# A graph network layer: eight buffers of gathered rows in place of six, and half the descriptor ring

## The chip, the cores and the metric

The kernel runs on one core of one Trainium2 chip. The metric is the device time of one execution in microseconds (us); a comparison rests on the median of several runs.

## The reference

One layer of message passing over 12500 nodes of 64 features and 412500 edges of 32 features, sorted by receiver. Cut to what is computed (`act` is `x * sigmoid(x)`):

```
h = maximum(layernorm(x), 0)
msg_in = concat(h[src], h[dst], edge)                  # 64 + 64 + 32 per edge
messages = act(msg_in @ W1 + b1) @ W2 + b2
logits = act(msg_in @ Wa1 + ba1) @ Wa2 + ba2
messages = messages * softmax(logits, axis=0)          # over all edges
aggregated = segment_sum(messages, dst)
out = x + act(concat(h, aggregated) @ Wu1 + bu1) @ Wu2 + bu2
```

## The kernel before

**Prologue.** The nodes are normalised in chunks, and two tables are written to memory: `ts_d`, each node's share of both first layers as a sender (128 numbers, 512 bytes a row), and `tr_d`, the same as a receiver. The stores of `tr_d` are L415; the sums ahead of them are the lines L412 on VectorE, from two tiles `tr` that take turns.

**Main loop (`one_pass`).** The edges, in order of their receivers, are cut into 403 groups of 1024 (eight columns of 128). `load(g)` runs two groups ahead of the group that is worked on. It fetches, on SyncE, a window of `tr_d` (tile `wins`, three buffers), and every fourth group edge features and receivers (`eo`, `dbs`), and computes with TensorE (L659) into PSUM `pe` what edge and receiver give. The senders' rows come by indirect DMAs of GpSimd, one for each column of 128 edges (L630), into a buffer `gs` of the pool `gather`. `begin(g)` adds `gs` to `pe` on VectorE (L678, and L680 or L682 for the last column) and applies tanh on ScalarE (L683); this reading is what frees the buffer. `end(g)` makes messages and logits, and `sum_up` adds up a group some iterations back (L764 copies its result out of PSUM).

Not every column is gathered by GpSimd. In the groups `chosen` (every even one from 10 to 390) ScalarE copies the senders' 128 columns one by one out of `hT` in SBUF (L570), in four parts of 32 over the two iterations that begin four before the group; the copies take their addresses from registers that are loaded from a list of byte addresses (L562). In the groups `rowed` (g mod 8 = 1, from 17 to 377) SyncE fetches the 128 rows one by one, 16 in each iteration (L600). Those groups have seven gathers, the others eight.

**What sets the order.** Nearly all instructions of the engines are pinned in the order in which the program writes them. The gathers are in the program's order on GpSimd's queue, and each waits for its buffer. As GpSimd has no other work, it runs ahead of the loop as far as buffers allow. The pool `gather` has six buffers of 4 KB per partition. The first two are taken before the loop by `raws`, the nodes' rows of groups 0 to 3, so groups 4 to 7 get the next four, groups 8 and 9 wait until `raws` is used up, and from group 10 on the gathers of group g wait for `begin(g - 6)`.

At the start of each SBUF partition lies the ring in which GpSimd writes the descriptors of its DMAs, 16 KB by default, and 128 bytes of constants; then comes `hT`, the first tile. `HOME = 16512` is therefore the byte address of `hT`, and the lists of addresses hold `4 * column + HOME`:

```
pin(nc.vector.tensor_scalar(to, to, 4.0, float(HOME), op0=ALU.mult, op1=ALU.add))
...
pin(nc.scalar.copy(to[:, at:at + 4], hb[:, bass.ds(regs[i] - HOME, 4)]))
```

**End.** The last groups have no columns by ScalarE and no single rows. Then the sums are turned into the update, whose inputs (`bs`, `xs`, L811 and L812) for the last five of 13 parts lie in buffers of the pool `gather` too.

Of the kernel before, what the change touches and what calls it, by code (L numbers as in the profile page):

```python
# [76 lines left out]
EVERY = 4  # L77
LEADS = {0: 8, 2: 8}
SLOTS = ((0, 32), (32, 32), (64, 32), (96, 32))
HOME = 16512  # L80
FIRST = 10
ROWS = 16
SPAN = -(-EP // ROWS)
# [16 lines left out]
def gnn_kernel(ctx: ExitStack, tc: tile.TileContext, n_edges, x, src, src_row, dst, dst_row, first, edge,  # L100
               weights, out):
    nc = tc.nc
# [90 lines left out]
    wrong = const.tile([EP, 1], I32, name="wrong")  # L193


    gather = ctx.enter_context(tc.tile_pool(name="gather", bufs=6))


    with tc.tile_pool(name="node1", bufs=1) as node1, \
# [281 lines left out]
def one_pass(tc, n_edges, v):  # L481
# [18 lines left out]
    with ExitStack() as ctx:  # L500
# [13 lines left out]
        with tc.tile_pool(name="work2", bufs=2) as work2, \  # L514
# [9 lines left out]
            def column_lists():  # L524

                m = NB // 2
                for i, (r, gs) in enumerate(of_phase.items()):
# [12 lines left out]
                    pin(nc.vector.scalar_tensor_tensor(to, to, float(P), near, op0=ALU.mult, op1=ALU.add))  # L540
                    pin(nc.vector.tensor_scalar(to, to, 4.0, float(HOME), op0=ALU.mult, op1=ALU.add))
                    pin(nc.vector.tensor_scalar(num, num, 1, None, op0=ALU.bitwise_and))
# [15 lines left out]
            def columns(g, first, n):  # L558
                if first == 0:
                    cols[g] = small.tile([P, EP], F32, name="cols", bufs=2)  # L560
                to = cols[g].bitcast(U8)
                loads, regs = nc.values_load_multi_w_load_instructions(  # L562
                    lists[g][0:1, first:first + n], engines=[ENG.Activation], min_val=HOME,
                    max_val=HOME + 4 * (NP // 2 - 1),
                    skip_runtime_bounds_check_because=WHY)
                for one in loads:
                    pin(one)
                for i in range(n):
                    at = 4 * (first + i)
                    pin(nc.scalar.copy(to[:, at:at + 4], hb[:, bass.ds(regs[i] - HOME, 4)]))  # L570

# [674 lines left out]
```

## Time and profile before

| | |
|---|---|
| median of 3 runs (lowest, highest) | 6093.8 us (6085.5, 6116.05) |
| profiled execution, as a whole | 6095.58 us |
| its span, first to last instruction | 6093.9 us |
| mean granted TensorE clock | 0.593 |
| busy: TensorE, VectorE, ScalarE, GpSimd | 38%, 47%, 52%, 47% |
| moved by DMA | 387.82 MB, 64 GB/s on average |

In the profile PE is TensorE's matmuls, PEld its weight loads, DVE VectorE, ACT ScalarE, POOL GpSimd, SP SyncE (SPq its queue). L630 is line 630 of the kernel. A group of instructions is told by its line, engine and operation, then "written tile <- tiles read". What stands behind "<-" in a wait is what the engine waited for last; "issue" is idle time in which it waited for nothing that the profile shows, and "remote" a release that the profile can't name.

### The profile page before, as it was taken

How to read it: one execution, taken by the hardware profiler on the slowest of the kernel's cores; microseconds unless marked ns; L12 is line 12 of the kernel's file. 1: busy time of each engine (PE TensorE's matmuls, PEld its weight loads, DVE VectorE, ACT ScalarE, POOL GpSimd, SP SyncE). 2: the span in 40 equal slices, each digit the busy share in tenths (PEclk: the TensorE clock that was granted, in tenths of full speed). 3: DMA queues.
4: the chain of work that ended last, by engine and by line, in shares of the span. 5: the costliest groups of instructions: out<-in, count | busy, mean ns of one | idle time of the engine just before them, and what ended most of it. 6: DMA issues, size and time to landing. Idle time of an engine off the chain costs nothing. (4 is left out here: it accounts for less than half of the span.)

```text
span 6093.9 us, 81385 instructions
## 1 busy us (share of the span) xinstructions
PE 2340.9 (38%) x11616; PEld 1926.1 (32%) x11616; DVE 2856.1 (47%) x6971; ACT 3176.7 (52%) x25258; POOL 2843.3 (47%) x3012
## 2 busy tenths in 40 slices
PE   4333334434333343344434433333333333333345
PEld 3333233323333232233323333332323322322334
DVE  4444444445444444445444444444444444444446
ACT  2455555555555555555555555555555555555531
POOL 4544444444444444445445444444444544444443
PEclk6666555555555555655556665566556666555656
DMA  4222222222222221222222222222222212122222
GB/s 172 66 68 53 61 59 62 68 56 66 62 59 63 53 67 52 66 56 67 62 53 70 56 68 55 62 63 53 66 56 62 65 52 57 53 53 60 61 72 67
DMA packets 238362, 387.82 MB, mean 64 GB/s; under 512 B 77789, under 2 KB 167368, under 8 KB 224760
## 3 DMA queue, kind: packets, MB, share of 16 engines
q1 hardware_dynamic: 142232, 187.67, 12.0%
q0 software_dynamic: 95584, 194.90, 11.8%
q14 instruction: 451, 3.69, 0.2%
q8 instruction: 95, 1.56, 0.1%
HBM read 359.56 MB, written 22.71 MB: 63 GB/s over the span
## 5 line engine op out<-in xcount | busy, mean ns | idle before, releaser
L630 POOL DMA_INDIRECT gs<-ts_d,src_sb x2955 | 2791.7, 945 | 3153.4 <-DVE ss L764 867.7
L570 ACT COPY cols<-hT 128x4 uint8 x24448 | 2691.3, 189 | 2522.8 <-issue 2489.0
L659 PE MATMUL pe<-wins,eo 128*128 128x256 f32 x3224 | 1459.5, 628 | 2472.2 <-DMA wins<-tr_d 1068.9
L659 PEld LDWEIGHTS pe<-wins,eo 128*128 128x128 f32 x3224 | 977.1, 319 | 2755.1 <-issue 1401.4
L764 DVE COPY ss<-sp 65x40 f32<-65x40 f32 x403 | 76.9, 191 | 1723.9 <-remote 1608.9
L758 PE MATMUL sp<-wt,acts 128*65 128x40 f32 x6448 | 600.8, 265 | 55.3 <-DVE wt L755 43.7
L758 PEld LDWEIGHTS sp<-wt,acts 128*65 128x65 f32 x6448 | 568.5, 181 | 61.8 <-DVE wt L755 47.4
L683 ACT ACTIVATE pe<-sm 128x1024 f32<-128x1024 f32 x403 | 409.3, 1016 | 206.8 <-DVE ss L764 102.4
L678 DVE TENSOR_TENSOR sm<-pe,gs 128x896 f32<-128x896 f32 (+1 forms) x399 | 455.1, 1141 | 33.8 <-issue 14.7
L723 PE MATMUL mt<-ident,mx 128*128 128x128 f32 x107 | 47.2, 441 | 926.4 <-DVE sums L787 765.5
L668 DVE SCALAR_TENSOR_TENSOR cols<-odd,half,cols 128x128 f32<-128x128 int32 x191 | 67.0, 351 | 666.5 <-ACT cols L570 585.6
L693 DVE SCALAR_TENSOR_TENSOR acts<-pe,sm 128x512 f32<-128x512 f32 x403 | 275.1, 683 | 180.9 <-ACT pe L683 118.9
L723 PEld LDWEIGHTS mt<-ident,mx 128*128 128x128 f32 x107 | 19.3, 180 | 937.7 <-remote 617.8
L701 DVE TENSOR_TENSOR pe<-pe,w_all 128x512 f32<-128x512 f32 x403 | 281.9, 699 | 13.4
L699 DVE SCALAR_TENSOR_TENSOR pe<-pe,sm 128x512 f32<-128x512 f32 x403 | 280.4, 696 | 10.6
L704 DVE TENSOR_REDUCE lg<-pe 128x8 f32<-128x512 f32 x403 | 277.3, 688 | 10.5
L655 DVE TENSOR_SCALAR eo<-dbs,bj 64x256 f32<-64x256 int32 x806 | 273.6, 369 | 17.2 <-DMA list_d<-to 7.6
L769 PEld LDWEIGHTS mt<-ss,w2u 65*128 65x128 f32 x806 | 206.9, 286 | 189.1 <-DVE gm L730 74.8
L769 PE MATMUL mt<-ss,w2u 65*128 65x40 f32 x806 | 181.9, 320 | 131.3 <-DVE gm L730 64.6
L755 DVE TENSOR_TENSOR wt<-sp,p 128x320 f32<-128x320 f32 x403 | 198.1, 492 | 13.8
L751 DVE TENSOR_TENSOR sp<-sp,dloc 128x320 f32<-128x320 f32 x403 | 200.1, 497 | 9.4
L783 DVE SCALAR_TENSOR_TENSOR sums<-sums,scale,mt 64x40 f32 x214 | 54.5, 255 | 235.4 <-PE mt L769 174.2
(137 smaller groups left out, 1233.0 us busy)
## 6 DMA issues: line engine op xcount, KB each, us to landing
single<-ts_d SPq DMA_DIRECT2D x5888, 0.5 KB
eo<-in_edge_dram SPq DMA_DIRECT2D x100, 512.0 KB
dbs<-in_dst_row_dram SPq DMA_DIRECT2D x200, 256.0 KB
gs<-ts_d,src_sb POOLq DMA_INDIRECT x2955
wins<-tr_d SPq DMA_DIRECT2D x806, 32.0 KB
odd<-list_d SPq DMA_DIRECT2D x191, 64.0 KB
ts_d<-ts SPq DMA_DIRECT2D x5, 896.0 KB
tr_d<-tr SPq DMA_DIRECT2D x5, 896.0 KB
```

Of the source, the lines that this page charges most:

```text
L570: pin(nc.scalar.copy(to[:, at:at + 4], hb[:, bass.ds(regs[i] - HOME, 4)]))
L630: nc.gpsimd.indirect_dma_start(out=full[:rows, j, :], out_offset=None, in_=ts_d[:, :], in_offset=bass.IndirectOffsetOnAxis(ap=src_full[:ro ...
L655: pin(nc.vector.tensor_scalar(eo[:WR, e], db[:, e], bj[g // NQ % 2 * WR:(g // NQ % 2 + 1) * WR, g, h:h + 1], None, op0=ALU.is_equal))
L659: pin(nc.tensor.matmul(pe[:, 2 * q:2 * q + 2, :], eo[:, q * EP:(q + 1) * EP], win[:, q // 2, :, :], start=True, stop=g >= RAW and (q < H - ...
L678: pin(nc.vector.tensor_tensor(sm[:, :n, :], pes[g][:, :n, :], gs[:, :n, :], ALU.add))
L683: pin(nc.scalar.activation(pes[g], sm, AF.Tanh))
L693: pin(nc.vector.scalar_tensor_tensor(acts[g % ACTS][:, :, 0:U], th[:, :, U:C], 1.0, gs[:, :, U:C], op0=ALU.add, op1=ALU.mult))
L699: pin(nc.vector.scalar_tensor_tensor(att, th[:, :, 0:U], 1.0, gs[:, :, 0:U], op0=ALU.add, op1=ALU.mult))
L701: pin(nc.vector.tensor_tensor(att, att, wa2[:EP, None, :].to_broadcast([EP, K, U]), ALU.mult))
L704: pin(nc.vector.tensor_reduce(lgs[s][:, k:k + K], att, AX.X, ALU.add))
L758: pin(nc.tensor.matmul(sp, acts[g % ACTS][:, j, :], wt[:, j, :], start=j == 0, stop=j == K - 1))
L769: pin(nc.tensor.matmul(pp, w2u.rearrange("s h u -> s (h u)"), sps.pop(g), start=True, stop=True))
```

## The change

The pool `gather` gets eight buffers. The 8 KB that this takes in each partition come from the descriptor ring, which is asked for with 8 KB in place of 16 KB. `hT` then starts 8 KB lower, and `HOME` follows. No instruction of the main loop is added, removed or moved; the waits of the gathers on their buffers follow the new count, and at the end some of the loads L811 and L812 are placed ahead of window loads on SyncE's queue. All lines from 81 on have a number that is higher by one.

```
-HOME = 16512
+RING = 8192
+HOME = RING + 128
...
-    gather = ctx.enter_context(tc.tile_pool(name="gather", bufs=6))
+    gather = ctx.enter_context(tc.tile_pool(name="gather", bufs=8))
...
-    nc = bacc.Bacc("TRN2", target_bir_lowering=False, num_devices=1)
+    nc = bacc.Bacc("TRN2", target_bir_lowering=False, num_devices=1,
+                   dynamic_dma_scratch_size=RING)
```

## The prediction

> **What bounds the kernel now.** I began with the page: its busy times and its costliest groups.
>
> ```profile
> PE 2340.9 (38%) x11616; PEld 1926.1 (32%) x11616; DVE 2856.1 (47%) x6971; ACT 3176.7 (52%) x25258; POOL 2843.3 (47%) x3012
> ...
> L630 POOL DMA_INDIRECT gs<-ts_d,src_sb x2955 | 2791.7, 945 | 3153.4 <-DVE ss L764 867.7
> L570 ACT COPY cols<-hT 128x4 uint8 x24448 | 2691.3, 189 | 2522.8 <-issue 2489.0
> L764 DVE COPY ss<-sp 65x40 f32<-65x40 f32 x403 | 76.9, 191 | 1723.9 <-remote 1608.9
> ```
>
> No engine is busy for more than 52% of the span. So the kernel is held up by waiting. Two large idle times have no producer's name: ScalarE (ACT) idles 2489.0 us at "issue" ahead of its small column copies, and VectorE (DVE) 1608.9 us at "remote" ahead of L764. The busy time of each engine in chosen stretches tells what goes on in them (first group of columns PE, then weight loads, DVE, ACT, POOL):
>
> ```profile
> core 0: us, PE busy (x) PEld busy (x) DVE busy (x) ACT busy (x) POOL busy (x), PEclk, DMA share, GB/s
> 152.00:182.00 30.00, 18.59 (x64) 13.57 (x63) 26.60 (x47) 16.07 (x16) 21.29 (x23) 0.79 0.44 106
> 184.00:204.00 20.00, 0.00 (x0) 0.00 (x0) 0.00 (x0) 4.97 (x33) 12.83 (x14) 0.56 0.17 49
> 5353.00:5366.00 13.00, 6.60 (x32) 5.53 (x32) 7.46 (x20) 9.71 (x91) 0.01 (x1) 0.63 0.22 54
> ```
>
> From 184 to 204 us POOL gathers, and TensorE (PE) and DVE do nothing at all; from 5353 to 5366 us POOL rests, and ACT issues 91 instructions in 13 us against 33 in 20. The timeline shows the same for SyncE, which issues sixteen row loads in 19.07 us beside gathers and in 5.14 us without them:
>
> ```profile
> 5334.30 19.07 SPq L600 DMA_DIRECT2D single<-ts_d  x16
> ...
> 5356.61 5.14 SPq L600 DMA_DIRECT2D single<-ts_d  x16
> ```
>
> So gathering nearly stops the other engines. It does not always: from 152 to 182 us POOL gathered for 21.29 us, and DVE was still busy for 26.60 of 30. Why it does so is open; for the forecast it counts when POOL gathers, not how many buffers there are. Whether the buffers themselves are short is seen from everything that touches the tile gs (durations in ns, first and last start, then who waited for it, us and times), and from POOL's waits (us in total, times, longest):
>
> ```profile
> L630 POOL DMA_INDIRECT gs<-ts_d,src_sb x2955: 938/944/1155, 73.9 to 5990.2; - x197
> L678 DVE TENSOR_TENSOR sm<-pe,gs x399: 1079/1092/1226, 169.9 to 6044.0; 128x896 f32<-128x896 f32 x191, 128x1024 f32<-128x1024 f32 x9
> ...
>   DVE sm L678: 1.6, 4
> ```
>
> ```profile
> POOL gs L630 <- DVE ss L764: 867.7, 82, 19.8
> ...
> POOL gs L630 <- DVE sm L682: 635.4, 84, 15.2
> POOL gs L630 <- DVE sm L680: 363.6, 35, 14.4
> POOL gs L630 <- DVE sm L678: 358.8, 48, 14.2
> ...
> POOL gs L630 <- DMA gs<-ts_d,src_sb: 40.5, 133, 0.3
> ```
>
> POOL waits 867.7 + 635.4 + 363.6 + 358.8 = 2225.5 us on DVE, that is for `begin` to free a buffer. But the reader L678 waited for gathered rows for 1.6 us in all: the last gather starts at 5990.2 us and the last use at 6044.0 us, 54 us apart. POOL is early, and it waits because it is early.
>
> **More buffers, main loop: nothing.** With eight buffers the gathers of group g+8 follow `begin(g)`, in place of those of g+6. The event that starts a burst is the same, and the order of instructions on the engines is unchanged in the loop. The 1.6 us that could be gained is all. What changes is which burst is short. A group has eight gathers if odd and seven if even, but of the odd groups every fourth (g mod 8 = 1, 46 of them: the 5888 row loads by 128) has seven. That short burst moves from iteration 3 of eight to iteration 1. One gather each way cancels, unless the two places differ; one gather is 1.25 us (two rows below), so 46 x 1.25 = 57.5 us is the most that either place can charge or give back. I take 0 and keep both ends for the range.
>
> **More buffers, before the loop: later.** Today POOL pauses here, since two of six buffers hold the raw rows of the first groups and groups 4 to 7 hold the rest:
>
> ```profile
> 112.79 0.94 POOL L630 DMA_INDIRECT gs<-ts_d,src_sb  x1 [0.30 <-issue]
> 151.54 0.94 POOL L630 DMA_INDIRECT gs<-ts_d,src_sb  x1 [37.81 <-ACT pe L683]
> 152.79 0.94 POOL L630 DMA_INDIRECT gs<-ts_d,src_sb  x1 [0.30 <-issue]
> ```
>
> The first gathers of groups 8 and 9 lose their waits on PE, ACT and DVE and follow at once: 16 gathers at 1.25 us (152.79 - 151.54), 20.0 us, to 133.7 us. This is the time in which the prologue ends. What it did under the gathers ahead of them, DVE's timeline shows:
>
> ```profile
> 84.89 0.96 DVE L412 TENSOR_TENSOR tr<-pn,w_all 128x768 f32<-128x768 f32 x1 [1.63 <-PE pn L311]
> 94.78 1.23 DVE L412 TENSOR_TENSOR tr<-pn,w_all 128x1024 f32<-128x1024 f32 x1 [8.93 <-remote]
> 114.39 0.96 DVE L412 TENSOR_TENSOR tr<-pn,w_all 128x768 f32<-128x768 f32 x1 [18.39 <-remote]
> ```
>
> DVE sat for 18.39 us and went on at 114.39 us, just after the last gather (112.79 + 0.94 = 113.7 us). Behind it are queued the remaining sums L412 and with them SyncE's stores of tr_d, the window loads and the first group's matmuls. If the stop lasts as long as the gathers, everything up to the first tanh comes 20.0 us later. Bounds: 0 (as from 152 to 182 us) and 20.0; I take 20.0, since 84 to 114 us is the same burst and the same work. In the first iterations POOL is then two groups further, with bursts as long as now: no term.
>
> **More buffers, the end: earlier.** The last two groups' gathers now follow `begin(393)` and `begin(394)`, where they followed `begin(395)` and `begin(396)`. The tanh L683 marks each iteration:
>
> ```profile
> 5971.30 1.03 ACT L683 ACTIVATE pe<-sm 128x1024 f32<-128x1024 f32 x1 [7.33 <-DVE sm L678]
> ...
> 5999.20 1.03 ACT L683 ACTIVATE pe<-sm 128x1024 f32<-128x1024 f32 x1 [1.03 <-DVE sm L678]
> ...
> 6028.66 1.03 ACT L683 ACTIVATE pe<-sm 128x1024 f32<-128x1024 f32 x1 [7.82 <-DVE sm L678]
> ...
> 6045.32 1.03 ACT L683 ACTIVATE pe<-sm 128x1024 f32<-128x1024 f32 x1 [5.93 <-DVE sm L678]
> ```
>
> Iterations 395 and 396, with 16 gathers, took 5999.20 - 5971.30 = 27.9 us; the last two, with none, 6045.32 - 6028.66 = 16.7 us. Gain 11.2 us; bounds 0 and the 20.0 us of the gathers. The last loads for the update (L811, L812) move ahead of some window loads on SyncE; what they wait for is long done by then, so 0.
>
> **The smaller ring: nothing.** It could only act through the time of a gather. That time can be had at the start, when the ring has taken 32 gathers, and deep in the loop:
>
> ```profile
> core 0: us, POOL busy (x), PEclk, DMA share, GB/s
> 73.00:114.00 41.00, 30.40 (x32) 0.55 0.32 108
> 400.00:5800.00 5400.00, 2531.56 (x2680) 0.59 0.23 60
> ```
>
> 30.40/32 = 0.950 us and 2531.56/2680 = 0.945 us: a ring that has been filled many times costs no more than one hardly used. And few are under way: each gather waits for the eighth before it to land, which cost POOL 40.5 us in 133 waits, 0.3 us at most. So at most eight are open, against several groups' worth of ring. I take 0; the lower bound is 0, since POOL's speed is not what ends last, the upper one the slowest gather, 1155 - 944 = 211 ns x 2955 = 624 us. The start value `HOME` moves with the ring, so the columns' addresses cost what they did.
>
> A rule that speaks against the ring's half: by the Trainium skill, Perfetto Trace Analysis, "DMA Instruction — SWDGE (GPSIMD)", DMA engines may start on a gather before its descriptors are all written, above all when these exceed the descriptor buffer. By that rule half a ring would sooner tie a gather to the pace at which rows land, and the sum would grow by the ring rival's price below; the median of 944 ns, and a worst of 1155, show no sign of it.
>
> **Sum.** 0 + 20.0 - 11.2 + 0 = +8.8 us on the profiled execution (span 6093.9 us, 6095.58 us as a whole, against a median of 6093.8 us, so 0.03% apart). 6093.8 + 8.8 gives 6103 us, 0.14% more: no change that can be told, for a measurement of this kernel tells about 0.5% (30 us).
>
> **Rivals.** *The prologue does not stop* (0.13): the 16 gathers run beside it, as from 152 to 182 us. 6093.8 - 11.2 = 6083 us. Against it stand the 18.39 us. The Trainium skill, SBUF — State Buffer, "Who interferes with whom", is on this side: only VectorE and GpSimd share a port there, and PE and ACT never wait on anyone; the 20 us in which PE did nothing and ACT crawled disagree. *Nothing changes at all* (0.08): both ends are hidden, 6094 us.
> *Slower, by the short burst* (0.18): iteration 3 pays for its eighth gather in full, and iteration 1, whose time is set by SyncE's row loads, gives nothing back. 6103 + 57.5 = 6160 us. It decides "slower" once 22 of the 57.5 us are not returned. For it: SyncE's sixteen loads cost 19.07 us beside gathers and 5.14 us else, so places do differ. Against: each pair of iterations has both kinds.
> *Faster, by the short burst* (0.16): iteration 1 gives back 57.5 us, iteration 3 hides its own: 6103 - 57.5 = 6045 us.
> *Slower, by the ring* (0.05): POOL waits for room. A tenth of the bound, 62 us, gives 6165 us, all of it 6727 us.
>
> **Numbers.** My forecast, 6103 us, has 0.40. Within 0.5%: 0.40 + 0.13 + 0.08 = 0.61; slower 0.18 + 0.05 = 0.23; faster 0.16. The likeliest case's own range is 6074 (no stop, all 20 us gained) to 6114 (20 us lost, nothing gained). The range reaches to both short-burst cases, 6040 to 6165, and leaves out the ring and their outer parts.
>
> **What would show it.** Right: a gather at about 114 us with no pause before it, the first tanh at about 170 us in place of 150, the last gather's lead on the last use of gathered rows longer than 54 us by about an undisturbed pair of iterations (16.7 us), gathers at 944 ns, and main-loop iterations of the same mean. Wrong: gathers over 0.95 us, or pauses of POOL inside a group (the ring); a first tanh near 150 us (no stop); a mean over iterations 1 to 4 of eight that differs by over 1 us (the short burst).

## The result and the profile after

The changed kernel took 6114.67 us (median of 20 runs, 6052.08 to 6167.73) against 6098.39 us (20 runs, 6034.12 to 6135.04) for the kernel before, run beside it. The ratio is 1.0126, with a 95% interval of 1.008 to 1.0173. The ratio leaves out, of each kernel, the runs that lie more than 1.5% above its fastest; the medians of all runs differ by 16.3 us, a factor of 1.0027. The profiled execution took 6086.03 us. So by its interval the kernel became slower, where I had forecast 6103 us and no change that can be told.

Of the page after: busy times, and the costliest groups.

```profile
PE 2344.0 (39%) x11616; PEld 1934.5 (32%) x11616; DVE 2857.8 (47%) x6971; ACT 3175.3 (52%) x25258; POOL 2843.5 (47%) x3012
...
L631 POOL DMA_INDIRECT gs<-ts_d,src_sb x2955 | 2793.3, 945 | 3127.0 <-issue 854.1
L571 ACT COPY cols<-hT 128x4 uint8 x24448 | 2690.1, 189 | 2487.2 <-issue 2449.3
L765 DVE COPY ss<-sp 65x40 f32<-65x40 f32 x403 | 76.9, 191 | 1667.3 <-remote 1582.3
```

Nothing in it has moved: the same work, 945 ns a gather, and the same nameless idle times of ACT and DVE. What touches the tile gs, as in the prediction, and what POOL then waited for (the same view, of POOL alone: us in total, times):

```profile
L631 POOL DMA_INDIRECT gs<-ts_d,src_sb x2955: 938/944/1797, 78.4 to 5964.0; - x197
L679 DVE TENSOR_TENSOR sm<-pe,gs x399: 1080/1092/1226, 197.0 to 6033.7; 128x896 f32<-128x896 f32 x191, 128x1024 f32<-128x1024 f32 x9
```

```profile
  issue: 864.3, 2708
  DVE sm L683: 812.6, 97
  DVE ss L765: 697.1, 69
  DVE sm L679: 371.3, 60
  DVE sm L681: 295.7, 29
  ACT pe L684: 39.2, 1
  DMA ts_d<-ts: 33.7, 1
  DVE stand L791: 12.2, 1
  DMA gs<-ts_d,src_sb: 4.6, 15
```

POOL still waits 812.6 + 697.1 + 371.3 + 295.7 = 2176.7 us for DVE to free a buffer (2225.5 before): it fills eight buffers as it filled six, and then waits. The last gather now leads the last use by 6033.7 - 5964.0 = 69.7 us, where it was 54.

The start, on the timelines of POOL, DVE and ACT:

```profile
110.91 0.94 POOL L631 DMA_INDIRECT gs<-ts_d,src_sb  x1 [0.30 <-issue]
...
138.39 0.94 POOL L631 DMA_INDIRECT gs<-ts_d,src_sb  x1 [0.30 <-issue]
178.53 0.94 POOL L631 DMA_INDIRECT gs<-ts_d,src_sb  x1 [39.20 <-ACT pe L684]
...
102.69 0.96 DVE L413 TENSOR_TENSOR tr<-pn,w_all 128x768 f32<-128x768 f32 x1 [8.64 <-remote]
139.09 1.22 DVE L413 TENSOR_TENSOR tr<-pn,w_all 128x1024 f32<-128x1024 f32 x1 [33.05 <-remote]
...
176.94 1.03 ACT L684 ACTIVATE pe<-sm 128x1024 f32<-128x1024 f32 x1
```

POOL does not pause at 112 us; it gathers on to 139.3 us. DVE sat for 33.05 us (18.39 before) and went on at 139.09, 0.2 us ahead of the last gather's end. The first tanh came at 176.94 us: 27.0 us later. Of these, 4.5 us lie ahead of the first gather of the loop, which started at 78.4 us where it started at 73.9. The end, on ACT's timeline:

```profile
5969.61 1.03 ACT L684 ACTIVATE pe<-sm 128x1024 f32<-128x1024 f32 x1 [8.62 <-DVE sm L679]
...
5988.94 1.03 ACT L684 ACTIVATE pe<-sm 128x1024 f32<-128x1024 f32 x1 [1.03 <-DVE sm L679]
```

Iterations 395 and 396 took 19.33 us, where they took 27.9.

### The profile page after: what moved, and what is told of

The parts are those of the page before. It is cut to its first block, busy times and chain, and to the rows that moved or that the text cites. A ratio compares the mean times of both kernels' runs of the same rounds, so it can differ in the third digit from the quotient of the medians.

```text
span 6084.2 us, 81382 instructions
## 1 busy us (share of the span) xinstructions
PE 2344.0 (39%) x11616; PEld 1934.5 (32%) x11616; DVE 2857.8 (47%) x6971; ACT 3175.3 (52%) x25258; POOL 2843.5 (47%) x3012
## 5 line engine op out<-in xcount | busy, mean ns | idle before, releaser
L571 ACT COPY cols<-hT 128x4 uint8 x24448 | 2690.1, 189 | 2487.2 <-issue 2449.3
L724 PEld LDWEIGHTS mt<-ident,mx 128*128 128x128 f32 x107 | 19.3, 180 | 953.4 <-remote 569.7
L656 DVE TENSOR_SCALAR eo<-dbs,bj 64x256 f32<-64x256 int32 x806 | 273.9, 370 | 18.0 <-DMA list_d<-to 8.1
L752 DVE TENSOR_TENSOR sp<-sp,dloc 128x320 f32<-128x320 f32 x403 | 199.8, 496 | 9.4
```

Source lines behind the costliest of these rows:

```text
L656: pin(nc.vector.tensor_scalar(eo[:WR, e], db[:, e], bj[g // NQ % 2 * WR:(g // NQ % 2 + 1) * WR, g, h:h + 1], None, op0=ALU.is_equal))
```

## The experiments

Three theories stood at first. **A**: the whole change lies at its two ends, the 16 gathers ahead of the first tanh and the last gathers two iterations earlier. **B**: the loop loses by itself. **C**: the smaller ring costs. Two questions came behind them: whether the change can be told from none at all, and what a gather does to the other engines.

The runs met two conditions. In some sets the kernel before took 6.10 to 6.15 ms, as in the forecast's profile; in others 3.90 to 3.92 ms. One and the same chip showed 3915, 3898 and, 33 minutes after the second of these, 6154 us, so this is not a property of a chip. Each run below is compared with the kernel before in its own set.

**The change again, the ring alone, two reserved buffers, four buffers.**

> The changed kernel once more, with eight buffers and the ring of 8 KB. Theory A, the order of the gathers: the whole change lies at the two ends, 16 gathers moved ahead of the first tanh (149.95 us before, 176.94 us in the first profile of the changed kernel, +27.0) and the last gathers two iterations earlier (iterations 395 and 396 took 27.9 us before and 19.3 us after, -8.6); the time is then 18 us above the kernel before, a ratio of 1.003, and the first tanh lies again at 170 to 180 us. Theory B, the loop: the ratio of 1.0126 is real in full, 77 us, of which 58 us are lost in the 400 iterations, 0.15 us each, whatever the two ends show; the ratio is 1.010 or more again.

The ring alone, against the kernel before:

```
-HOME = 16512
+RING = 8192
+HOME = RING + 128
...
+                   dynamic_dma_scratch_size=RING)
```

> The kernel before with six buffers, and of the change only the ring of 8 KB with the address that follows from it. Theory A: nothing happens; first tanh at 150 us, iterations 395 and 396 at 28 us, a gather 945 ns, ratio 1.000. Theory C, the ring: half as many descriptors stand ready, so POOL waits for places in some bursts; gathers above 950 ns or gaps between gathers of one burst, and most of the change's 1.0126 is here (ratio 1.008 or more).

Two reserved buffers, against the changed kernel:

```
+        held = [gather.tile([P, K, C], F32, name="gs") for _ in range(2)]
```

> The changed kernel with two of its eight buffers reserved at the start without use, so that groups 8 and 9 again take the buffers of the input rows and wait for them as in the kernel before; from group 10 on there are eight buffers. Theory A: the first tanh goes back from 177 to 150 us (152 at most 157), the end stays as in the changed kernel (iterations 395 and 396 at 19.3 us), and the time is 9 us below the kernel before (ratio 0.9985) and 27 us below the changed kernel (0.9955 of it). Theory B, the loop: the start goes back as well, but the loop keeps its loss of 58 us; ratio to the kernel before 1.008.

Four buffers, against the kernel before:

```
-    gather = ctx.enter_context(tc.tile_pool(name="gather", bufs=6))
+    gather = ctx.enter_context(tc.tile_pool(name="gather", bufs=4))
```

> The kernel before with four buffers in place of six, ring of 16 KB: the step of the change in the other direction. Theory A: the 16 gathers of groups 6 and 7 wait for the buffers of the input rows, so the first tanh comes 20 to 27 us earlier (123 to 130 us), the last gathers come two iterations later (iterations 395 and 396, or the pair after them, 8 to 11 us longer), the lead of the last gather over its use falls from 54 us to about 26 us, and nothing waits for rows: 10 to 18 us below the kernel before, ratio 0.997 to 0.998. Rival, the rows come late: with two groups queued instead of four, the addition of the gathered rows waits for them in the pair that follows a pair of groups; each wait of 2 us in 200 pairs is 400 us, and the ratio is 1.02 or more.

This set fell in the other condition: the kernel before took 3915.42 us (35 runs). The ratios were: the change 1.0008 (0.9999 to 1.0016), the ring alone 1.0000 (0.9992 to 1.0009), two reserved buffers 1.0007 (0.9998 to 1.0015), four buffers 1.0000 (0.9991 to 1.0008). Theory C falls here. The ring alone did not run in the other condition, but the profile after speaks for it there: the gathers of the changed kernel are as long as before (945 ns), and inside a group POOL never pauses for more than 0.4 us; nor does it in the three profiles of the slower condition with half the ring that come below. The reserved buffers brought no wait: their profile has groups 8 and 9 following at once, so that kernel counts as one more run of the change.

Why so little happens shows in stretches of the loop's beginning, here of the ring alone (span 3912.8 us) and of the change again (3916.3 us); columns as in the prediction:

```profile
180.00:220.00 40.00, 23.76 (x120) 19.13 (x119) 31.89 (x81) 34.96 (x322) 30.23 (x33) 0.66 0.38 93
```

```profile
200.00:240.00 40.00, 24.42 (x124) 19.71 (x122) 30.54 (x79) 33.97 (x303) 30.25 (x33) 0.63 0.38 91
```

POOL gathers all through (33 gathers in 40 us), and ACT issues 322 or 303 instructions, PE 120. In the prediction's stretch from 184 to 204 us ACT issued 33 in 20 us and PE none. In this condition these rows show no engine that a gather holds, and so its place should have next to no price. The first tanh lay at 101.82 us with the ring alone and at 103.51 us with the change.

**The kernel before once more; the change a third time; four reserved buffers; no gathers.** In this set the kernel before took 6136.36 us (17 runs).

> The kernel before, unchanged, once more under its own name: what two sets of runs of one program differ by, and its profile on the chip of these runs. The ratio is 1.000, and an interval that leaves 1.000 out would say that an interval of this kind is too narrow for differences of some tenths of a per cent. Where the loop takes 9.5 us an iteration, as in the first four experiments, the first tanh is at 102 us and POOL is between gathers most of the time; where it takes 14.8 us, as in the profile from which the forecast was made, it is at 150 us.

> The changed kernel a third time. Theory A, the order of the gathers: where the kernel before takes 6.1 ms, +18 us (1.003), first tanh 27 us later, iterations 395 and 396 8.6 us shorter; where it takes 3.92 ms, no engine stops while POOL gathers, so the same 16 gathers ahead of the first tanh cost nothing: 1.000 to 1.001. Theory B, the loop: 1.010 or more where the kernel before takes 6.1 ms.

> The changed kernel with four of its eight buffers reserved at the start without use: the gathers of groups 6 to 9 wait for the buffers of the input rows, and from group 10 on there are eight buffers. Theory A: where the kernel before takes 6.1 ms, the 32 gathers stand no longer ahead of the first tanh, which comes 20 to 27 us earlier than in the kernel before (123 to 130 us), the end stays as in the changed kernel (-8.6 us), and the time is 29 to 36 us below the kernel before (ratio 0.995). Where it takes 3.92 ms: 0.999 to 1.001, as every other number of buffers. Theory B, the loop: ratio above 1.005 where the kernel before takes 6.1 ms.

No gathers, against the changed kernel:

```
+            zero = gather.tile([P, K, C], F32, name="gs")
+            nc.gpsimd.memset(zero, 0.0)
...
-                full = None if g < RAW else gather.tile([P, K, C], F32, name="gs")
+                full = None if g < RAW else zero
...
-                for j in range(0 if g < RAW else K - (g in chosen or g in rowed)):
+                for j in range(0):
```

> The changed kernel without its 2955 gathers of the loop: every group adds one buffer of zeros (the gathered rows are missing from the result), all other work stays. Theory D, the gathers hold the other engines: the loop's iteration falls from 14.8 us to what ACT, DVE and the queues need by themselves, 9 us or less, where the kernel before takes 6.1 ms (to some 3.7 ms); where it takes 3.92 ms, the iteration of 9.5 us moves by 0.5 us at most (3.7 to 3.92 ms), since POOL is then 94% occupied but its rows lie 20 to 60 us ahead of their use. Rival: POOL's order of 8.9 us an iteration (7.3 gathers of 0.945 + 0.27 us) is what bounds the faster case, and the iteration falls to DVE's 7.1 us (3.0 ms).

The kernel before against itself gave 6157.77 us (12 runs) and 1.0063, with an interval of 1.0015 to 1.0111. The interval leaves 1.000 out, so it is too narrow for what it is asked here; by the medians of all runs the same kernel differs from itself by 21.4 us, a factor of 1.0035. The change gave 6200.2 us (6 runs), 1.0183 (1.0123 to 1.0243), by the medians 1.0104; four reserved buffers, again without the wait that I wanted (first tanh at 174.95 us), 6183.33 us (6 runs) and no ratio, by the medians 1.0077.

Without the loop's gathers the kernel took 3883.2 us (4 runs), a ratio of 0.6369 (0.6331 to 0.6406). Its page:

```profile
span 3883.7 us, 76653 instructions
...
PE 2239.8 (58%) x11616; PEld 1865.4 (48%) x11616; DVE 2792.7 (72%) x6971; ACT 2894.9 (75%) x25258; POOL 53.3 (1%) x58
```

So the gathers cost 6136 - 3883 = 2253 us here, 0.76 us each, though almost nothing ever waits for their rows: theory D, that gathers hold the other engines. (That the condition held for these four runs too is taken from the other 41 of the set, none of which took less than 6.05 ms.) By the tanhs an iteration lasts 9.35 us without them. The rival, 7.1 us, falls.

**Waits put back at the start, narrow rows, POOL busy without DMA.** Here the kernel before took 3914.07 us (21 runs). All four are edits of the changed kernel. The wait ahead of group 8; in the second run 6 stands in place of 8:

```
+                if g == 8:
+                    for raw in v["raws"]:
+                        pin(nc.gpsimd.memset(raw[0:1, 0, 0, 0:1], 0.0))
...
-                    nc.gpsimd.indirect_dma_start(
+                    one = nc.gpsimd.indirect_dma_start(
...
+                    if g < 8 + 2:
+                        pin(one)
```

> The changed kernel, in which POOL clears one element of each of the two buffers of input rows ahead of the gathers of group 8, so that groups 8 and 9 wait at the start as in the kernel before (the two reserved buffers of the third experiment did not bring this wait: groups 8 and 9 followed there without a pause). From group 10 on eight buffers. Theory A, where the kernel before takes 6.1 ms: first tanh at 150 us (as before, 27 us ahead of the changed kernel), iterations 395 and 396 at 19.3 us as in the changed kernel, time 9 us below the kernel before. Theory B, the loop loses by itself: the start goes back and the ratio stays at 1.005 or more. Where the kernel before takes 3.92 ms: first tanh at 102 us, 1.000.

> As f1_wait8, with the wait ahead of group 6: only the 16 gathers of groups 4 and 5 stand ahead of the first tanh. Theory A, where the kernel before takes 6.1 ms: the first tanh comes 20 to 27 us ahead of the kernel before (123 to 130 us), iterations 395 and 396 at 19.3 us, time 29 to 36 us below the kernel before (0.995). Rival: the gathers that are held at the start run in the first iterations of the loop instead and hold those for as long, so the tanh of group 12 comes no earlier than in the kernel before, and the time is -9 us as in f1_wait8. Where the kernel before takes 3.92 ms: 1.000.

Narrow rows; the buffers are a quarter as wide too, eight of them under a name of their own, and the addition reads each row four times over:

```
-                        out=full[:rows, j, :], out_offset=None, in_=ts_d[:, :],
+                        out=full[:rows, j, :], out_offset=None, in_=ts_d.rearrange("n (q c) -> (n q) c", q=4),
```

> The changed kernel with as many gathers of 128 rows each, but of 128 bytes a row in place of 512 (other rows, a quarter of the data; the addition repeats them four times, so the result is not the reference's). Theory D1, the number of gathers and their descriptors holds the other engines: the loop's iteration stays at 14 to 15 us where the kernel before takes 6.1 ms. Theory D2, their data does, in the DMA engines: the part of the iteration above the 9.4 us of the kernel without gathers falls to a quarter, 5.2 to 1.3 us, so 10.7 us and a time of 4.4 ms. Where the kernel before takes 3.92 ms: 9.4 to 9.5 us by both.

A memset in place of each gather:

```
-                    nc.gpsimd.indirect_dma_start(
-                        ...
+                    nc.gpsimd.memset(full[:rows, :, :], 0.0)
```

> The changed kernel with each of the 2955 gathers of the loop replaced by a memset of the group's buffer on POOL (128x1024, estimated at 0.95 us from 0.205 us for 128x128 and 0.10 us for 128x1): POOL is busy as long and in the same order, but issues no DMA (the gathered rows are missing from the result). Theory D3, a busy POOL holds the others by itself, through a port or a semaphore: the iteration stays above 13 us where the kernel before takes 6.1 ms. Theory D1 or D2: it falls to 9.4 us, 3.88 ms.

The waits gave 1.0009 both (1.0000 to 1.0018). Narrow rows took 3895.74 us (one run): 18 us less, which tells nothing of D1 and D2 where nothing is held. The memsets took 4133.99 us (one run), 220 us more, which no theory had; D3 itself was asked of the slower condition and stays open. Rows of that profile, POOL's and DVE's:

```profile
L631 POOL MEMSET gs<- 128x1024 f32 x2955 | 2823.7, 959 | 1145.1 <-DVE sm L677 950.1 <-PE pe L663 49.8 <-DVE lg L703 2.0
...
L654 DVE TENSOR_SCALAR eo<-dbs,bj 64x256 f32<-64x256 int32 x806 | 769.1, 983 | 16.8 <-DMA dbs<-in_dst_row_dram 7.6
L789 DVE COPY stand<-nmax 64x40 f32 x806 | 488.0, 605 | 4.0 <-issue 0.9
...
L677 DVE TENSOR_TENSOR sm<-pe,gs 128x896 f32<-128x896 f32 x237 | 256.1, 1081 | 0.0
...
L750 DVE TENSOR_TENSOR sp<-sp,dloc 128x320 f32<-128x320 f32 x403 | 230.8, 573 | 9.5
```

The comparisons L654 take 983 ns where they take 368 with the gathers (the change again, L656), the copies L789 605 where they take 195; the additions take 1081, as with the gathers (1087). So work of POOL's that writes SBUF stretches some operations of DVE, and gathers, as long on POOL, stretch none. The Trainium skill, SBUF — State Buffer, "Who interferes with whom", says that copies and tensor_scalar can run in modes that hold a port pair which DVE shares with GpSimd, and that a tensor_tensor has no such mode and contends only with GpSimd's reads, when both its inputs lie in SBUF. The first three rows of DVE agree. The comparisons L750, with one input in SBUF and one in PSUM, do not quite: 573 ns on the mean beside memsets, which only write, and 497 beside gathers (L752 of the change again).

The waits and the narrow rows then ran again in further sets, and the wait ahead of group 6 in a last one:

> f1_wait8 again (the changed kernel, groups 8 and 9 wait at the start as in the kernel before). Theory A, where the kernel before takes 6.1 ms: first tanh at 150 us, iterations 395 and 396 at 19.3 us, time 9 us below the kernel before. Theory B, the loop loses by itself: ratio 1.005 or more with the first tanh at 150 us. Where the kernel before takes 3.92 ms: 1.000 to 1.001 again.

> f2_wait6 again (only the gathers of groups 4 and 5 ahead of the first tanh). Theory A, where the kernel before takes 6.1 ms: first tanh at 123 to 130 us, iterations 395 and 396 at 19.3 us, time 29 to 36 us below the kernel before. Rival: the held gathers run in the first iterations and hold those as long; the tanh of group 12 then comes no earlier than in the kernel before, and the time is 9 us below it. Where the kernel before takes 3.92 ms: 1.000 to 1.001 again.

> e9_narrow again (as many gathers of 128 rows, a quarter of the bytes; other rows are added than the reference's). Theory D1, the number of gathers and descriptors holds the others: 14 to 15 us an iteration where the kernel before takes 6.1 ms. Theory D2, their data does: 10.7 us, 4.4 ms. Where the kernel before takes 3.92 ms: 3.90 ms again.

> f2_wait6 once more (only the gathers of groups 4 and 5 ahead of the first tanh). Theory A, where the kernel before takes 6.1 ms: first tanh 20 to 27 us ahead of the kernel before (123 to 130 us), iterations 395 and 396 at 19.3 us, 29 to 36 us below the kernel before. Rival: the held gathers hold the first iterations as long; the tanh of group 12 comes no earlier than in the kernel before, -9 us. Theory B: the loop loses whatever the start does, ratio 1.005 or more.

> e9_narrow once more (as many gathers, a quarter of the bytes; other rows are added than the reference's). Theory D1, number of gathers and descriptors: 14 to 15 us an iteration where the kernel before takes 6.1 ms. Theory D2, data: 10.7 us, 4.4 ms.

> f2_wait6 a last time. Theory A, where the kernel before takes 6.1 ms: first tanh at 123 to 130 us, 29 to 36 us below the kernel before. Rival: the held gathers hold the first iterations as long; the tanh of group 12 comes no earlier than in the kernel before, -9 us. Theory B: the loop loses whatever the start does, ratio 1.005 or more. Where the kernel before takes 3.9 ms: 1.001, the 3 to 5 us that eight buffers cost there in four of four kernels, and that the kernels with six and four buffers did not show.

Beside a kernel before of 3898.47 us the waits gave 1.0013 (1.0004 to 1.0021) and 1.0006 (0.9998 to 1.0015), and narrow rows 3879.34 us. Beside one of 3914.37 us the wait ahead of group 6 gave 1.0012 (1.0003 to 1.0021), and narrow rows 3893.36 us. The last run met the slower condition, beside a kernel before of 6154.01 us (17 runs): 6181.99 us (12 runs), ratio 1.0052 (0.9957 to 1.0147), by the medians 1.0045. Its POOL and ACT on the timeline:

```profile
85.43 0.95 POOL L634 DMA_INDIRECT gs<-ts_d,src_sb  x1 [0.30 <-issue]
117.83 0.09 POOL L631 MEMSET gs<- 1x1 f32 x1 [31.46 <-PE pe L670]
126.25 0.09 POOL L631 MEMSET gs<- 1x1 f32 x1 [8.32 <-PE pe L670]
126.93 0.96 POOL L634 DMA_INDIRECT gs<-ts_d,src_sb  x1 [0.59 <-issue]
...
124.44 1.03 ACT L689 ACTIVATE pe<-sm 128x1024 f32<-128x1024 f32 x1
...
155.18 1.03 ACT L689 ACTIVATE pe<-sm 128x1024 f32<-128x1024 f32 x1 [11.47 <-DVE sm L684]
181.65 1.03 ACT L689 ACTIVATE pe<-sm 128x1024 f32<-128x1024 f32 x1 [1.37 <-DVE sm L684]
202.86 1.03 ACT L689 ACTIVATE pe<-sm 128x1024 f32<-128x1024 f32 x1 [20.19 <-DVE sm L684]
...
317.68 1.02 ACT L689 ACTIVATE pe<-sm 128x1024 f32<-128x1024 f32 x1
```

The wait does what it should: POOL stops after group 5, and the first tanh comes at 124.44 us, 25.5 us ahead of the kernel before. Then the held gathers run, and the two iterations behind 155.18 us take 26.5 and 21.2 us; in the same kernel's profile of the other condition they took 6.4 and 5.7 us. The tanh of group 12 comes at 317.68 us: later than before, not earlier. The rival named in its expectation is right on this, and theory A has to be put in another way. The 9 us below the kernel before, which the rival had too, did not come: the time is not shown to differ.

## Why the prediction was right or wrong

The six profiles of the slower condition give one account. Times are starts of tanhs, in us; the gathers are those of the loop that started ahead of the tanh of group 12:

| | before | before once more | change | change, third | four reserved | wait ahead of group 6 |
|---|---|---|---|---|---|---|
| first tanh | 149.95 | 153.23 | 176.94 | 170.39 | 174.95 | 124.44 |
| tanh of group 12 | 295.95 | 301.60 | 320.75 | 318.93 | 321.55 | 317.68 |
| gathers started by then | 114 | 114 | 129 | 129 | 129 | 129 |
| from there to group 395 | 5675.4 | 5738.5 | 5648.9 | 5720.3 | 5792.1 | 5807.9 |
| iterations 395 and 396 | 27.9 | 28.6 | 19.3 | 19.3 | 19.3 | 19.3 |

The rows of the two group-12 tanhs of the profile before and the profile after:

```profile
295.95 1.02 ACT L683 ACTIVATE pe<-sm 128x1024 f32<-128x1024 f32 x1
```

```profile
320.75 1.02 ACT L684 ACTIVATE pe<-sm 128x1024 f32<-128x1024 f32 x1
```

**Prologue: right in mechanism and size, and charged to the wrong thing.** I said that 16 gathers follow at once and stop the work for 20.0 us. They did, and three profiles with eight buffers and no added wait have the first tanh 17 to 27 us later than the two before. Part of that spread lies ahead of the loop's first gather, which starts anywhere from 70.8 to 78.4 us; counted from it, the first tanh comes after 98.6 to 99.6 us in these three and after 76.1 and 78.2 us in the two before, 22 us apart. Yet the price does not belong to the place. With the wait ahead of group 6 the first tanh came earliest of all, and at group 12 that kernel stood where the other three stand: 317.7 to 321.6 us against 296.0 and 301.6, 21 us apart on the mean. Eight buffers let POOL run two groups further ahead. By the tanh of group 12, 129 gathers have started in all four, 114 in both before; whenever these 15 run, they hold the others, 1.4 us each. The rival "the prologue does not stop" falls by the 33.05 us.

**End: right, a little large.** I expected 11.2 us back; 8.6 came in the first profile, and 8.9 on the mean of the columns above (28.3 against 19.3 us). I took iterations with no gathers as the measure for 16.7 us; these two last 19.3 us without gathers.

**Ring: right.** 944 ns a gather at the median, as forecast, and no pause inside a group. Four of 2955 took longer than the worst of before, 1797 ns at most, together some 2 us more than four usual ones; the kernel before once more, with the whole ring, has three such, up to 1721 ns, so they are not the ring's.

**Main loop: this is the step that failed, as far as can be told.** I put the loop at zero and closed with "no change that can be told", for which I took 0.5% (30 us) as the bound; the ratio came out at 1.0126, with an interval that lies above that bound. What should stand in place of the zero stays open. The two ends gave 21 - 8.9 = +12 us, where my sum was +8.8; in the profiles of the change, all that lies outside the stretch from group 12 to group 395 takes 12.6 us more than in those of the kernel before. The medians of the first comparison say +16, which leaves 4 us to the loop. The ratio says some 77 us, which would leave 65; but with the change at its median of 6114.67 us it would put the kernel before at 6038.6 us, and only two of that kernel's 20 runs are as low. The later sets with eight buffers lie 28 to 64 us above the kernel before by their medians, where the kernel before lies 21 us above itself. So the sign is the same each time, and it is on the slower side; I had given that 0.23.

The profiles show no such loss in the loop, and cannot exclude it. From group 12 to group 395 the change took 5648.9 and 5720.3 us, the kernel before, in the same sets, 5675.4 and 5738.5; the two other kernels with eight buffers took 5792.1 and 5807.9, in executions of 6230.09 and 6242.23 us, well above their medians. The two profiles of the kernel before alone differ by 63 us. The rivals of the short burst have no support: by position in the eight, from group 16 to group 384, the mean of iterations 1 to 4 was 14.30 us before and 14.29 us after, and 14.78 and 14.76 us in the later pair, and the criterion was a difference of 1 us. Single positions can't be read: iteration 3 lasted 17.76 us in one profile of the kernel before and 12.01 us in the other.

The bound of 0.5% was the second fault. The kernel before against itself came out at 1.0063, outside it; a forecast of +8.8 us could not be told from one of +30 us in this condition. The wait ahead of group 8, which would part start from loop most directly, met only the condition in which nothing is held, so theory B stays open there. In that condition eight buffers gave 1.0006 to 1.0013 in all seven comparisons, and six and four buffers 1.0000: 2 to 5 us lost, though five of the seven intervals reach 1.000. The kernels that wait at the start show it too, so it isn't the start's; its cause wasn't looked into. No kernel with all of the reference's work beat the kernel before.

## What to carry to other kernels

Ask of a buffer whether anyone waits for what it holds: where POOL is 54 us early and the readers waited 1.6 us in all, more buffers only let it be early sooner, and if its work holds the other engines, that is paid at the start and only partly given back at the end. A stop that moves from one place to another is no gain; follow the account to a milestone that lies behind both places (here the tanh of group 12), not to the first that gets better. And compare a kernel with itself before an interval of half a per cent is believed, and look whether the medians of all runs say the same.

## What the runs showed of the hardware

One program, the kernel before, had two speeds, 3.89 to 3.92 ms and 6.03 to 6.25 ms, on the same chip within an hour. They differ in what a running gather does to the other engines. In the slower one, while POOL gathers, ACT, SyncE, PE and DVE nearly stop. Over the 111 long bursts of the profile before (14 or more gathers with at most 0.6 us between two, from 400 to 5800 us), ACT started on the mean 5.6 to 9.2 instructions in each of the first five us of a burst, 0.5 to 2.3 in each of the eleven behind them, and was back at 4.1 and 9.9 in the third and fourth us behind the burst's end. From the tenth us on PE started 0.1 and DVE 0.4 or fewer in a us; whether they stop by themselves or for want of what ACT and SyncE bring is not shown. With half the ring, after, ACT falls off at the same point (7.3 in the fifth us, 2.5 in the sixth). The gathers themselves take 945 ns in both, and DVE's operations last as long in both (the additions of 896 columns 1087 ns). The page rows of ACT's copies show it in one line each, for the change again and, in the section on the result, for the profile after: 189 ns a copy in both, but 505.0 us idle ahead of them in one and 2487.2 us in the other.

```profile
L571 ACT COPY cols<-hT 128x4 uint8 x24448 | 2402.8, 189 | 505.0 <-issue 480.9
```

Taking the gathers out brings the slower condition to 3883 us, under the faster one's 3915 us with them: a gather costs 0.76 us of the whole in one and about 0.01 us in the other. The granted TensorE clock was lower in the profiles of the slower one, 0.58 to 0.60 against 0.65 to 0.66 (0.63 with the memsets), but 0.65 without the gathers beside the slower one: the low clock comes with the gathers there, and whether it is a cause or follows from the stops no run tells. What sets the condition, and whether it is the number of gathers, their data or a busy POOL that holds the engines, is open: all runs made for it met the faster one.
